# The last step of a graph layer: attention sums in other banks, products by graph, products of ones by ones, and a new written order

## The chip, the cores and the metric

The kernel runs on one core of one Trainium2 chip. The metric is the device time of one execution in microseconds (us); the figure quoted is the median of several runs. Engines are named as the profile names them: PE is TensorE's matmul, PEld its weight load, DVE is VectorE, ACT is ScalarE, POOL is GpSimd and SP is SyncE. L1054 means line 1054 of the kernel.

## The reference

There are 128 graphs of 128 nodes with 1024 features each, all in float32. A layer has two parts, and both add to the features.

```python
def gnn(h, adj, W, a):                       # h: layer norm of x; 16 heads of 64
    Wh = heads(h @ W)
    e = leaky_relu(Wh @ a[:F] + Wh @ a[F:])  # one number for each row and head
    att = softmax(where(adj == 0, -9e15, e)) * adj
    return elu(att @ Wh)

def ffn(x, router_w, down, up):              # x: layer norm again
    gates = softmax over the two largest of (x[:, 0, :] @ router_w.T)   # 8 experts
    d = einsum('blh,erh->bler', x, down)     # rank 16 for each expert
    return x + einsum('bler,ehr,be->blh', d, up, gates)

x = x + gnn(layernorm(x), adj, adj, W, a)
x = x + ffn(layernorm(x), router_w, down, up)
```

Each graph chooses its two experts by its first row alone. The attention weight of a row does not depend on the column except through the mask, so a product with the adjacency matrix followed by a factor for each row and head gives the attention's output.

## The kernel before, in words

**Stages.** Graphs are worked in 64 pairs and in 32 groups of four. The big product with `W` is done for a pair at a time, by a scheme of seven block products named M1 to M7 (a Strassen-like scheme; `a` and `b` behind the name are its column halves). They add up in two double banks of PSUM, `pw0` and `pw1`, which `slot_of(0)` and `slot_of(1)` hand out in turn. For two pairs together, the products with two of the blocks are split once more into inner products, with the code names J0 to J7 and I0 to I7 (L640). DVE and ACT read the banks (`u2`, `u4`, `c21`, `c22`) and POOL adds sums (`ps0` to `ps3` are the sums of a pair's transposed blocks that the next products take as one operand; `eo` and `f` are two more sums).

After the big product come, for each graph, the attention sums (product of `parts` with the adjacency, L770 or, at the end, L1054), the weighing by row (`sums`), the part above zero (`above`), an exponential on ACT and the part below zero (`below`). The graph is then transposed, and the features of a group of four go to the experts: gather the chosen rows of the lower factors (`fe0` to `fe8`, on POOL, L971), lower products (`D`, L986), their gating (`dn`), upper products (`U0` and `U1` for the two halves of the features, L1006) and the final adds (`v...`, L1015), whose results are written out.

**The order.** The kernel runs under a manual schedule: each engine executes its instructions in the order in which the program issues them. That order is written by hand in four lists of codes, FIRST, EVEN, ODD and LAST, one code for a small step. `between` runs a list for a step `q`; a code with `-` belongs to the step before, a code with `+` to the step behind. LAST is the order of the last step, which ends the big product of the last pair and then does all that remains. Moving a code moves all the instructions that it issues, on whatever engine, past the other codes' instructions on the same engines.

**The end.** `at_the_end` (L1039) defines the codes with `+` in LAST. The last two graphs (`i` and `i+1`) are done by halves of the features, so that one half can follow the other from engine to engine. With `r` the graph and `h` the half, the codes are these.

| Code | Function | Engine | What it does |
|---|---|---|---|
| A`rh` | `attend_half` | PE, L1054 | attention sums, two products of 512 columns |
| w`rh`, a`rh`, b`rh` | `weigh_half`, `above_half`, `below_half` | DVE | `sums`, `above`, `below` |
| E`rh` | `exp_half` | ACT | exponential of the sums |
| n`r`, q`r`, s`r` | `mean_of_halves`, `squares_at_end`, `stats_at_end` | POOL, ACT, POOL | mean, squares and deviation of the second layer norm |
| T`rh` | `turn_half` | PE, L1106 | four transposes of 128 columns |
| k`rh`, P`rh` | `keep_half`, `parts_of_half` | ACT, DVE | copy of the transposed half to `y_t`; its first row times the router |

The last group's four graphs go to the experts in two sets. Set A holds the group's first two graphs, which are finished earlier; set C holds the last two. All experts' lower factors are loaded once (`down_all`), so no gather is needed. With `s` the set, `t` the graph in it and `h` the half:

| Code | Function | Engine | What it does |
|---|---|---|---|
| P`s`, R`s` | `parts_of`, `sum_parts` | DVE | product of the first rows with the router, and its sum along the free axis |
| rd`s` | `devs_of` | POOL | the deviations as an operand |
| L`s`, V`s` | `logits_of`, `dev_of` | PE | sums over partitions by a product with ones: logits and deviations |
| ch`s`, sp`s` | `choose_of`, `spread_of` | DVE | the two largest logits, and their difference |
| rt`s`, wg`s` | `ratio_of`, `gates_of` | ACT, DVE | softmax of the two, and the gates |
| d`s` (before: dA, d0C, d1C) | `down_of` | PE, L1210 | lower products, all experts |
| g`s` | `gate_of` | DVE | gating (`dn`) |
| u`ths` | `up_of` | PE, L1224 | upper product, 512 columns |
| m`ths`, v`ths` | `scale_up` and `add_of_scaled` (set A), `add_of_up` (set C) | ACT and POOL, or DVE | scale by the deviation, add to the features, write out |

The steps `m..B` and `v..B` (L1237) do the same scaling and adding for the group before. `aw`, `pe` and `dw` make the attention weights of the two graphs, `join` and `rj` (`rejoin`, L849) put a graph's transposed halves into `y_t`.

**Banks at the end.** Beside `pw0` and `pw1` there is the pool `ps_d` with two double banks. `double` takes one, and waits until the readers of the one that it replaces are done; `single` takes one half of a double. In the kernel before, `attend_half`, `logits_of` and `down_of` all take from `ps_d`; the transposes of half `h` of both graphs go to `slot_of(h)`.

Of the kernel before, what the change touches and what calls it, by code (L numbers as in the profile page):

```python
# [8 lines left out]
F32 = mybir.dt.float32  # L9
# [5 lines left out]
ALU = mybir.AluOpType  # L15
# [32 lines left out]
Jt2- n0- hi0- lo0- J7- J1- q0- ps3- Jt3- Jp- y1- ro1- Jr- I1- n1- t0- J2- Jd- sr- q1- ps2-  # L48
J5- It0- J4- st1- Ja- Js- st0- M7b- J3- It1- M7a- Ip- rj0- Je- rp- c22- I6- ss- L- It2- ch0-
hi3- I7- t1- ch1- It3- fr- M4a- fe4- M4b- jn1- Ir- fe0- c21- lo3- hi2- fe5- Ia- I4- ra- rs-  # L50
fe2- I5- fe1- I2- fe7- Is- I3- lo2- A1 Ie- fe6- Id- hi1- fe3- aw M1b lo1- M1a jn0- pe LW+
# [12 lines left out]
def adj_ffn_kernel(  # L64
# [974 lines left out]
    def at_the_end():  # L1039
# [10 lines left out]
        def attend_half(r, h):  # L1050
            if i + r not in PH:
                PH[i + r] = double("ph")
# [47 lines left out]
        def turn_half(r, h):  # L1100
            if h not in turned:
                turned[h] = slot_of(h)
            pt = turned[h][:, r].rearrange("p (c n) -> p c n", c=CPH)
            for c in range(CPH):
                k = h * CPH + c
                nc.tensor.transpose(pt[:, c], X[i + r][:, k * P:(k + 1) * P], ident)  # L1106

        def keep_half(r, h):
            nc.scalar.copy(y_of(i + r)[:, h * CPH:(h + 1) * CPH],
                           turned[h][:, r].rearrange("p (c n) -> p c n", c=CPH))  # L1110
# [20 lines left out]
        def parts_of_half(r, h):  # L1131
            k = slice(h * CPH, (h + 1) * CPH)
            part = prod_of("C")[:, r:r + 1, :, k]
            rows = turned[h][:, r].rearrange("p (o c n) -> p o n c", o=1, c=CPH)[:, :, 0:1]
# [336 lines left out]
```

## Time and profile before

| What | Value |
|---|---|
| Four runs | 1858.46, 1858.52, 1859.89 and 1861.21 us |
| Median | 1859.21 us |
| Profiled execution, its own time | 1858.78 us |
| Its span | 1856.7 us |
| Mean granted clock of PE | 0.997 |
| Busy: PEld | 1504.7 us (81%) |
| Bytes read and written in HBM | 194.24 and 68.17 MB |

The span goes from the first instruction to the last; the execution's own time contains a little more. In the page's second part, the span is cut into 40 equal slices, and each digit is a busy share, or the granted clock of PE (`PEclk`), in tenths, where 9 stands for nine tenths or more. One slice is 46 us long, so the last digit averages over all that comes after the last big product and some of what lies ahead of it. Parts and groups of instructions are given by line, with the output and the operands by the program's names. In a timeline, a row that covers several records of one kind gives their start, their total length and their number, and in brackets the idle time of the engine ahead of them and what ended it. Tables of stretches give, for each stretch of the span, its length, then the busy time of one engine with the number of its instructions, the granted clock, the DMA engines' share and the GB/s that they moved.

### The profile page before, as it was taken

The page shows a single profiled execution, that of the slowest core. Times are in us where ns is not written, and L with a number is a line of the kernel's source. Part 1 is how long each engine was busy: PE and PEld are TensorE (multiplying, and loading weights), DVE is VectorE, ACT ScalarE, POOL GpSimd, SP SyncE. Part 2 cuts the span into 40 slices and gives each one's busy share as a digit, 9 for nine tenths or more (in the row PEclk, how much of TensorE's full clock was granted, in tenths as well). Part 3 has the DMA queues.
Part 4 walks back from the last instruction along what each step waited for, and adds up shares of the span by engine and source line. Part 5 has one row for each costly group of instructions (what it writes and reads, how often), then busy time and mean ns, then how long its engine had stood idle before and what let it go on. Part 6 is the DMA issues. An engine that isn't in the chain of part 4 may idle for free.

```text
span 1856.7 us, 29668 instructions
## 1 busy us (share of the span) xinstructions
PE 1839.3 (99%) x10196; PEld 1504.7 (81%) x10196; DVE 1580.0 (85%) x3411; ACT 1242.5 (67%) x1423; POOL 1170.4 (63%) x1691
## 2 busy tenths in 40 slices
PE   9999999999999999999999999999999999999997
PEld 6888888888888888888888888888888888888884
DVE  6888888888888888888888888888888888888885
ACT  3666666766666766666666667666667666666676
POOL 3666656667566667566666566675666675666663
PEclk9999999999999999999999999999999999999998
DMA  8455566565575655666655655655665556565443
GB/s 319 153 176 139 186 199 177 184 181 148 183 198 189 182 152 166 194 184 195 175 138 187 199 177 184 179 150 182 194 194 182 148 171 192 184 194 176 134 158 114
DMA packets 349100, 330.42 MB, mean 178 GB/s; under 512 B 279196, under 2 KB 281372, under 8 KB 348440
## 3 DMA queue, kind: packets, MB, share of 16 engines
q1 hardware_dynamic: 331512, 287.09, 51.1%
q0 software_dynamic: 17008, 40.91, 7.4%
q8 instruction: 81, 1.33, 0.3%
q14 instruction: 67, 0.55, 0.1%
q10 hardware_dynamic: 432, 0.53, 0.1%
HBM read 194.24 MB, written 68.17 MB: 141 GB/s over the span
## 4 chain that ended last, share of the span: by engine, by line
PE 92%; POOL 3%; DMA 1%; DVE 1%; issue 1%; ACT 1%; SPq 0%; DVEq 0%; POOLq 0%; ACTq 0%
PE pw L561 58%; PE pw L640 17%; PE ph L770 6%; PE pu L1006 4%; PE pd L986 3%; PE ix L640 3%; POOL down L971 2%; DMA xn<-in_x 1%; DMA w_sb<-in_w 1%; PE pd_all L1210 0%; POOL xt L493 0%; PE pu L1224 0%; ACT ph L802 0%; POOL s L493 0%; PE pl L899 0%
## 5 line engine op out<-in xcount | busy, mean ns | idle before, releaser
L561 PE MATMUL pw<-w_sb,xt 128*128 128x260 f32 (+1 forms) x4080 | 958.6, 385 | 1.0 <-DMA w_sb<-in_w 0.5
L561 PEld LDWEIGHTS pw<-w_sb,xt 128*128 128x128 f32 x4080 | 762.6, 190 | 169.5 <-issue 30.9
L971 POOL DMA_INDIRECT down<-table,at_down x248 | 249.0, 1004 | 197.2 <-DVE of_slot L935 116.0
L708 ACT ACTIVATE parts<-wh,rstd 128x512 fp32r<-128x512 f32 x192 | 135.2, 720 | 344.2 <-DVE wh L568 305.0
L849 ACT COPY y_t<-tt 128x2048 uint16<-128x2048 uint16 x126 | 314.7, 2498 | 1.4 <-DMA tt<-halves 1.4
L561 PE MATMUL pw<-w_sb,s 128*128 128x260 f32 (+1 forms) x1088 | 249.8, 382 | 0.0
L843 ACT COPY halves<-xn 128x2048 uint16<-128x2048 uint16 x126 | 237.5, 1885 | 2.5 <-DVE xn L793 2.0
L561 PEld LDWEIGHTS pw<-w_sb,s 128*128 128x128 f32 x1088 | 206.4, 190 | 34.1 <-DVE wh L568 0.9
L493 POOL TENSOR_TENSOR s<-xt 128x512 f32<-128x512 f32 x64 | 83.2, 1299 | 231.8 <-DMA xt<-in_x_t 231.8
L786 ACT ACTIVATE ph<-ph 128x1024 f32<-128x1024 f32 x126 | 127.9, 1015 | 82.3 <-DVE xn L783 78.7
L1015 DVE SCALAR_TENSOR_TENSOR xn<-pu,rstd,xn 128x512 f32<-128x512 f32 x244 | 168.7, 743 | 11.1 <-PE pu L1006 11.1
L776 DVE TENSOR_TENSOR ph<-ph,att 128x1024 f32<-128x1024 f32 x126 | 149.1, 1228 | 11.1 <-PE ph L770 4.9
L432 DVE BATCH_NORM_STATS2 stats<-xn 128x6 f32<-128x512 f32 x248 | 158.4, 680 | 0.0
L855 ACT ACTIVATE xn<-xn,off,mul 128x1024 f32<-128x1024 f32 x128 | 157.7, 1232 | 0.1
L793 DVE SCALAR_TENSOR_TENSOR xn<-ph,xn 128x1024 f32<-128x1024 f32 x126 | 153.2, 1216 | 0.2
L783 DVE SCALAR_TENSOR_TENSOR xn<-ph,xn 128x1024 f32<-128x1024 f32 x126 | 148.1, 1215 | 0.1
L802 ACT ACTIVATE ph<-xn,acc 128x1024 f32<-128x1024 f32 x126 | 140.9, 1118 | 8.2 <-POOL acc L798 6.3
L712 DVE SCALAR_TENSOR_TENSOR parts<-wh,rstd,parts 128x512 fp32r<-128x512 f32 x192 | 140.3, 744 | 4.2 <-ACT parts L708 0.5
L770 PE MATMUL ph<-parts,adj_f 128*128 128x512 f32 x504 | 142.1, 423 | 0.0
L640 PE MATMUL pw<-w_in,s 128*128 128x260 f32 x496 | 129.2, 383 | 0.0
L640 PE MATMUL pw<-w_sb,i 128*128 128x260 f32 x496 | 129.2, 383 | 0.0
L770 PEld LDWEIGHTS ph<-parts,adj_f 128*128 128x128 f32 x504 | 92.6, 188 | 24.3 <-issue 6.3
(235 smaller groups left out, 2678.3 us busy)
## 6 DMA issues: line engine op xcount, KB each, us to landing
xn<-in_x SPq DMA_DIRECT2D x128, 512.0 KB
xt<-in_x_t SPq DMA_DIRECT2D x127, 512.0 KB
out_y<-xn SPq DMA_DIRECT2D x124, 512.0 KB
adj_f<-in_adj_t POOLq DMA_DIRECT2D x32, 256.0 KB, 7.3
adj_i<-in_adj SPq DMA_DIRECT2D x32, 256.0 KB
down<-table,at_down POOLq DMA_INDIRECT x248, 2.6
w_sb<-in_w SPq DMA_DIRECT2D x3, 1040.0 KB
wt_sb<-in_w_t SPq DMA_DIRECT2D x1, 2048.0 KB
```

Source lines behind the costliest of these rows:

```text
L432: nc.vector.bn_stats(st[:, h, :], X[i][:, h * HALF:(h + 1) * HALF])
L561: nc.tensor.matmul(banks[name][:, j, cols], lhs()[:, k, :], w_sb[:, rhs, k, j, cols], start=(fresh and k == 0), stop=(k == KH - 1), skip_g ...
L640: nc.tensor.matmul(bank(name), sums(lhs)[:, k], w_of[rhs][:, k], start=(fresh and k == 0), stop=(k == KI - 1), skip_group_check=not fresh)
L770: nc.tensor.matmul(PH[i][:, h], GRP[g]["adj_f"][:, t, :], PARTS[q][:, s, NH * (i % 2) + h], start=(s == 0), stop=(s == 1))
L776: nc.vector.tensor_tensor(ph, ph, ATT[i // 2, None][:, i % 2, :, None].to_broadcast([P, H, F]), ALU.mult)
L783: nc.vector.scalar_tensor_tensor(X[i], whole(i), 0.0, X[i], op0=ALU.max, op1=ALU.add)
L793: nc.vector.scalar_tensor_tensor(X[i], whole(i), 1.0, X[i], op0=ALU.min, op1=ALU.add, accum_out=acc[:, 0:1])
L843: nc.scalar.copy(halves, X[i].bitcast(U16).rearrange("p (d s) -> p s d", s=2))
L849: nc.scalar.copy(y_of(i).bitcast(U16).rearrange("p k (n s) -> p s k n", s=2), TT.pop(i).rearrange("p (s k) n -> p s k n", s=2))
L855: nc.scalar.activation(X[i], X[i], AF.Identity, bias=GRP[g]["off"][:, t:t + 1], scale=GRP[g]["mul"][:, t:t + 1])
L971: nc.gpsimd.indirect_dma_start(out=st["down"][:, j * R:(j + 1) * R].rearrange("p r k -> p (r k)"), out_offset=None, in_=table, in_offset=b ...
L1015: nc.vector.scalar_tensor_tensor(y[:, cols], st["pu", h][t], st["rstd"][:, t:t + 1], y[:, cols], op0=ALU.mult, op1=ALU.add)
```

## The change

Five things are changed, all in the last step.

- The attention sums of the last two graphs go to `slot_of(0)` and `slot_of(1)`, where the big products' banks are, and not to the pool `ps_d`. The transposes go to one slot for each graph, not one for each half.
- Logits, deviations and lower products of a set share one double bank: for set A from `ps_d`, for set C `slot_of(0)`. The deviations lie in the second half of it, behind the logits.
- The lower products of set A are issued by graph (`d0A`, `d1A`, 128 columns each) and not for both together (`dA`, 256 columns).
- Two new codes issue products of a matrix of ones by itself (128 columns), whose results nobody reads: `y0+` six of them into the bank that the first transposes take, and `yA+` eight into the bank that the first upper product takes.
- The final adds of set A's second graph are done by DVE in one instruction each, as those of set C are, and not by ACT and POOL. The comparison that makes `hit` moves from the gates to the choice.

The list LAST is written anew with these codes. The order of the inner products, of POOL's gathers and pair sum `ps2`, of M4 and M7 against the lower products D, and of nearly all steps behind them is another one. The lists FIRST, EVEN and ODD stay.

```diff
 LAST = """
-Jt2- n0- hi0- lo0- J7- J1- q0- ps3- Jt3- Jp- y1- ro1- Jr- I1- n1- t0- J2- Jd- sr- q1- ps2-
-J5- It0- J4- st1- Ja- Js- st0- M7b- J3- It1- M7a- Ip- rj0- Je- rp- c22- I6- ss- L- It2- ch0-
...
-aw2 fe8- p1 A0 h1 M2a x1 M2b h0 rj1- x0 e1 eo y1 hi0 sc0 e0 lo0 y0 M6b M6a wg n1 q1 D t0 u2
-u4 f n0 hi1 dn aw0+ lo1 M7a M7b LR+ q0 pe0+ c22 U0 M4b ss t1 hi3 M4a dw0+ v00 rj0 v01 rdA+
-U1 m1B+ lo3 v1B+ m0B+ c21 aw1+ rj1 A00+ pe1+ hi2 A01+ w00+ w01+ v0B+ A11+ a01+ dw1+ a00+
-E01+ jn1 b01+ m2B+ PA+ w11+ lo2 RA+ E00+ T01+ A10+ m3B+ b00+ w10+ n0+ LA+ OA+ a11+ a10+ q0+
-s0+ E11+ VA+ T00+ dA+ E10+ chA+ k00+ b10+ spA+ b11+ k01+ T10+ T11+ n1+ v3B+ rtA+ wgA+ P11+
-k11+ P10+ gA+ u00A+ q1+ P0+ m00A+ RC+ v2B+ LC+ u01A+ jn0 s1+ rdC+ chC+ VC+ m01A+ v00A+ v01A+
-k10+ d1C+ spC+ rtC+ ac u10A+ d0C+ m10A+ wgC+ gC+ u11A+ j1+ u00C+ m11A+ u10C+ j0+ v10A+ u01C+
-v10C+ v00C+ u11C+ v11C+ v01C+ v11A+
+Jt2- Jt3- ps3- hi0- J7- lo0- J1- y1- Jp- J2- ro1- Jr- J4- J5- Jd- sr- t1- st0- n1- M7a- n0-
+Js- It0- J3- Ja- q1- It1- I1- Je- M7b- st1- t0- rp- I6- It2- q0- I7- Ip- ss- It3- L- I2-
...
+fe6- fe0- h0 x0 h1 e0 eo rs- M6a sc0 LR+ hi0 fe4- M6b wg fe3- y0 n0 ps2- lo0 t0 x1 M7b u2 u4
+M7a fe5- e1 q0 f y1 hi1 A00+ c22 aw0+ M4a lo1 t1 n1 hi3 pe0+ q1 lo3 dw0+ M4b c21 A01+ w01+
+OA+ aw1+ w00+ ss D hi2 dn a01+ rj0 a00+ E01+ U0 lo2 v01 A10+ b01+ E00+ pe1+ dw1+ b00+ A11+
+y0+ rdA+ v00 T01+ rj1 U1 w11+ PA+ n0+ T00+ m0B+ m1B+ q0+ RA+ w10+ LA+ k00+ k01+ d1A+ a11+
+v0B+ a10+ E11+ VA+ v1B+ b11+ E10+ m3B+ d0A+ b10+ chA+ T10+ spA+ n1+ T11+ jn1 P10+ m2B+ yA+
+P0+ ac rtA+ q1+ P11+ RC+ wgA+ s1+ gA+ s0+ LC+ u11A+ u01A+ k11+ rdC+ u10A+ k10+ chC+ d0C+ j1+
+v10A+ VC+ spC+ v2B+ jn0 rtC+ u00A+ m00A+ v00A+ v11A+ m01A+ d1C+ v3B+ wgC+ gC+ u10C+ u11C+
+u01C+ v10C+ j0+ u00C+ v00C+ v11C+ v01A+ v01C+
 """.split()
...
         def attend_half(r, h):
             if i + r not in PH:
-                PH[i + r] = double("ph")
+                PH[i + r] = slot_of(r)
...
         def turn_half(r, h):
-            if h not in turned:
-                turned[h] = slot_of(h)
-            pt = turned[h][:, r].rearrange("p (c n) -> p c n", c=CPH)
+            if r not in turned:
+                turned[r] = slot_of(r)
+            pt = turned[r][:, h].rearrange("p (c n) -> p c n", c=CPH)
...
+        def banks_of(s):
+            if ("banks", s) not in got:
+                got["banks", s] = double("banks") if s == "A" else slot_of(0)
+            return got["banks", s]
...
         def logits_of(s):
             n = sets[s][1]
-            got["pl", s] = double("pl")
-            nc.tensor.matmul(got["pl", s][:, 0, 0:n * E], ones, add_of(s)[:, 0:n * E], start=True,
+            nc.tensor.matmul(banks_of(s)[:, 1, 0:n * E], ones, add_of(s)[:, 0:n * E], start=True,
                              stop=True)
...
         def down_of(s, t, n):
-            if ("pd", s) not in got:
-                got["pd", s] = double("pd_all")[:, 0]
             first = sets[s][0] + t
             for k in range(KC):
-                nc.tensor.matmul(got["pd", s][:, t * P:(t + n) * P],
+                nc.tensor.matmul(banks_of(s)[:, 0, t * P:(t + n) * P],
...
+        def stay(n, idle):
+            for _ in range(n):
+                nc.tensor.matmul(idle, ones, ones, start=True, stop=True)
+
+        def stay_before_turn(n):
+            turned[0] = slot_of(0)
+            stay(n, turned[0][:, 0, 0:P])
+
+        def stay_before_up(n):
+            got["pu", "A", 0, 0] = single("pu")
+            stay(n, got["pu", "A", 0, 0][:, 0:P])
...
-        for t in range(2):
-            for h in range(2):
-                does.update({f"m{t}{h}A": (scale_up, "A", t, h)})
+        for h in range(2):
+            does.update({f"m0{h}A": (scale_up, "A", 0, h)})
...
-                    does.update({f"u{t}{h}{s}": (up_of, s, t, h), f"v{t}{h}{s}": (add_of_scaled if s == "A" else add_of_up, s, t, h)})
+                    does.update({f"u{t}{h}{s}": (up_of, s, t, h), f"v{t}{h}{s}": (add_of_scaled if s == "A" and t == 0 else add_of_up, s, t, h)})
```

More of the change, by code (lines that the diff above doesn't have):

```diff
@@ L1133, in parts_of_half @@
             part = prod_of("C")[:, r:r + 1, :, k]
[L1134 removed]
+            rows = turned[r][:, h].rearrange("p (o c n) -> p o n c", o=1, c=CPH)[:, :, 0:1]
             nc.vector.tensor_tensor(part, rows.to_broadcast(part.shape),
@@ L1155, in dev_of @@
             n = sets[s][1]
-            nc.tensor.matmul(got["pl", s][:, 1, 0:n], ones, add_of(s)[:, n * E:], start=True,
+            nc.tensor.matmul(banks_of(s)[:, 1, n * E:n * E + n], ones, add_of(s)[:, n * E:], start=True,
                              stop=True)
@@ L1181, in choose_of @@
             nc.vector.tensor_tensor(pr[:, 0], top[:, 1], top[:, 0], ALU.subtract)
+            hit = got["hit", s] = small.tile([P, n * TOP], F32, tag="own" + s, name="hit", bufs=1)
+            nc.vector.tensor_scalar(hit, val[:, 0].rearrange("p g s -> p (g s)"), own_order, None,
+                                    op0=ALU.is_equal)
         def spread_of(s):
             pr = got["pr", s]
-            nc.vector.tensor_tensor(pr[:, 0], pr[:, 0], got["pl", s][:, 1, 0:sets[s][1]], ALU.mult)
+            n = sets[s][1]
+            nc.vector.tensor_tensor(pr[:, 0], pr[:, 0], banks_of(s)[:, 1, n * E:n * E + n], ALU.mult)
         def ratio_of(s):
@@ L1197, in gates_of @@
             nc.vector.tensor_mul(gate[:, :, 1], pr[:, 1], gate[:, :, 0])
-            val = val.rearrange("p v g s -> p v (g s)")
-            hit = small.tile([P, n * TOP], F32, tag="own", name="hit", bufs=2)
-            nc.vector.tensor_scalar(hit, val[:, 0], own_order, None, op0=ALU.is_equal)
-            nc.vector.tensor_tensor(hit, hit, val[:, 1], ALU.mult)
+            hit = got["hit", s]
+            nc.vector.tensor_tensor(hit, hit, gate.rearrange("p g s -> p (g s)"), ALU.mult)
             gates = got["gate", s] = small.tile([P, n], F32, tag="gate" + s, name="gate_all", bufs=1)
```

18 lines of the change are left out of this document (10 added, 8 removed).

## The prediction

> **What bounds the kernel now.** I read the page first, for the engine that fills the span and for the chain of work that ended last.
>
> ```profile
> PE 1839.3 (99%) x10196; PEld 1504.7 (81%) x10196; DVE 1580.0 (85%) x3411; ACT 1242.5 (67%) x1423; POOL 1170.4 (63%) x1691
> ...
> PEclk9999999999999999999999999999999999999998
> ...
> PE 92%; POOL 3%; DMA 1%; DVE 1%; issue 1%; ACT 1%; SPq 0%; DVEq 0%; POOLq 0%; ACTq 0%
> ```
>
> The matrix engine is the bound for the whole span but its end. The change touches the last step alone, so the second view is the timeline of PE from 1820 us on (start, length, instruction, idle time before it and its releaser).
>
> ```profile
> 1819.74 0.61 PE L1006 MATMUL pu<-up,dn 32*128 32x512 f32 x4
> 1821.70 1.20 PE L1054 MATMUL ph<-parts,adj_f 128*128 128x512 f32 x4 [1.35 <-ACT part_up L1237]
> 1824.37 1.19 PE L1054 MATMUL ph<-parts,adj_f 128*128 128x512 f32 x2 [1.47 <-DVE sums_of L1060]
> 1827.03 1.11 PE L1106 MATMUL pw<-ident,xn 128*128 128x128 f32 x4 [1.47 <-DVE xn L1079]
> ...
> 1830.76 5.31 PE L1210 MATMUL pd_all<-y_t,w_sb 128*128 128x256 f32 x16
> 1835.90 1.04 PE L1106 MATMUL pw<-ident,xn 128*128 128x128 f32 x8
> 1837.70 1.10 PE L1224 MATMUL pu<-w_sb,dn_all 128*128 128x512 f32 x2 [0.76 <-PE pw L1106]
> ...
> 1846.60 4.46 PE L1224 MATMUL pu<-w_sb,dn_all 128*128 128x512 f32 x10
> ```
>
> Up to 1820.35 PE has no gap; after it come three waits of 1.4 us, and a block of 16 lower products that takes 5.3 us. The third view says why those are slow: PE in stretches of 3.41 us (busy, granted clock).
>
> ```profile
> 1820.51:1823.92 3.41, 1.20 (x4) 1.00 0.19 77
> 1823.92:1827.33 3.41, 1.50 (x4) 0.50 0.57 231
> 1827.33:1830.75 3.42, 3.42 (x14) 0.50 0.00 0
> 1830.75:1834.16 3.41, 3.41 (x10) 0.50 0.00 0
> 1834.16:1837.57 3.41, 2.78 (x17) 1.00 0.09 37
> ```
>
> After a stretch with 1.20 us of products (35%) the clock is 0.50 for 10.24 us. A stretch with 2.78 us, 1.9 of them not transposes, keeps it. So at most some 36 us of 1856.7 are open: from 1820.35 to the end. 0.2% is 3.7 us, about what a measurement of this kernel can tell from no change.
>
> **Part 1, up to the last big product.** The order of PE, DVE, ACT, POOL and SP in the built program says who stands behind whom. The inner products (0.88 us a pair of matmuls, by the chain) are reordered: the second joint product now comes right behind the first, and waits for ACT's copy of it (0.38 us) without the filler that stood between, 0.45 us. All that follows fits without a gap, and M6 (s2) ends at 1808.6 as before, since the first attention product of the old order (0.93) is merely elsewhere. M7 may start if pair sum `ps2` is there: on POOL that now stands behind seven gathers, where it was early. A gather takes 1.26 us from start to start; the chosen rows are known at 1794.5, and `eo` (1.30) and the rstd pair (1.0) are in between: `ps2` ends at 1808.4, 0.25 us ahead of need. If the gathers take the 1.42 us of the first one, M7 is 0.9 us late; I take none.
>
> M7 takes 3.70, A00 (half of the 0.93) 0.47, and M4 waits 0.27 for c22's read (0.70), where U0 used to fill. M4 ends at 1816.8, against 1819.27: D (2.16) and U0 (1.07) went behind it. That attention sums now live in pw0 and pw1, not in ps_d, allows this: A00 waits only for M6's readers (done at 1810).
>
> **Part 2, DVE from M4 to the second graph's last half.** From here DVE is laid end to end, at start-to-start distances of the timeline: c21 0.70, sums 0.65, five weights 0.90, sums 0.65, two above 1.28, `lo` 0.72, two L1015 1.36, below 0.75, four divisions 0.88, below 0.75, two L1015 1.36, sums 0.65, product 0.37, reduce 0.30, sums 0.65, two above 1.28: 13.25, to 1830.1. ACT comes out equal: from D's end (1819.4) dn 0.35, y_t 2.5, two exps 1.2, exp 0.2, y_t 2.5, two scalings 1.28, squares 1.25, two copies 1.05, exp 0.56, to 1830.35. Two below (1.5) end at 1831.9.
>
> PE in that time waits for DVE: U0 ends at 1820.9, A10 and A11 start at 1821.75 (behind `lo`), and U1's second half stands behind DVE's fourth L1015, to 1826.8. Lower products of graph A: 32 records of 128 columns in two lots of 16, each 1.8 (the chain's 1.78 for such a lot at full clock), with the logits (0.25) and deviations (0.3): from 1828.2 to 1832.3. Split by graph they cost what 16 records of 256 columns cost at full clock, so the split is free; the clock is not.
>
> **Part 3, choice to end.** The choice of A waits for the end of the last lower product, not of its logits, but DVE is busy to 1831.9 anyway: 0.45 us. Twelve small instructions at 0.2 (`hit` is now the twelfth, and leaves the part behind the exps, so it costs nothing in sum) 2.3, spread 0.17, product parts of C 0.95 (in their shade ACT's two, 0.45), four gates 0.8, dn 0.42: the first upper product starts at 1837.0, against 1837.70. Before, the choice ran beside the lower products; that is where most of the gain from the clock goes.
>
> Then PE: three upper at 0.86 (4.31 us for ten records) to 1839.6, lower 1.8, deviations 0.35, upper 0.86, lower 1.8 to 1844.4. DVE's second add of graph 1 (0.70), which was ACT's and POOL's, waits for ACT's scaling and has C's gates (0.8) and dn (0.42) queued behind it: the last four upper products start at 1845.2, 0.8 late, and end at 1848.7. Three adds of 0.68 follow: 1850.8. The last write: DVE's end to the span's end was 1852.51 to 1856.7, 4.2; as many writes are in flight, so 1855.0.
>
> **The ones products.** Six before the first transposes and eight before the first upper product. A record of 128 columns is 0.11 us at full clock: 12 records 1.3, 16 records 1.8. The first lot runs from 1822.7 to 1824.0, and `below` is ready at 1823.8; U1's second half waits to 1826.8, so it costs nothing. The second needs a bank that ACT frees at 1833.5 and ends at 1835.3, before DVE's reduce at 1835.8: nothing. At half clock they take 2.7 and 3.5 (the opening idle products took 3.97 us for 18, 0.22 each), and the second then delays the logits of C.
>
> **Sum.** 1855.0 is 1.7 below the span of 1856.7. The profiled execution took 1858.78 (2.08 around the span), 0.43 less than the median of 1859.21: 1857.1 for it, 1857.5 as a median.
>
> **Where the clock may still fall.** Behind the first lot of ones come a transpose (0.45), U1's first half (0.55), 1.8 of wait, U1's second half (0.55), a transpose (0.45). A stretch of 3.41 us from 1824.0 holds 1.1 us of products and 0.47 of transposes: between the 35% that fell and the 56 to 81% that did not. Where the stretches begin differs from run to run.
>
> The Trainium skill, "TensorE: Matmul & The Clock Gate", Part 4 (PE-mode transpose), says that a transpose does not count as busy work for the clock gate. By that rule the stretch has 32%, below the row that fell, and the ones stand ahead of the gap that matters: the clock would fall and the time be 1860.6; by the row alone (46%) it stays open. No run here has shown it. The same page, Part 1, gives the window as 3413 ns, which is the grid that the trace shows.
>
> **Rivals.**
> 1. The clock falls once, near 1827.5, and comes back two stretches later at 1834.3, as before: the lower products lose 3.1 us, all on the path. 1860.6. For it: the 35% row and the gap. Against: three of the waits before it are gone.
> 2. Slower: the same fall, but no stretch full enough until 1841, since the stretches in between hold transposes, small products and the wait for a bank. Then the lower products end at 1836.6, the eight ones products run at half clock from 1838.6 to 1842.1, and the logits of C, behind them on PE, come 6 us late; the choice of C decides the end. 1863 to 1866 if the clock is half until the upper products. It decides from the point where the ones end behind DVE's reduce. For it: in the profile a stretch that PE filled (3.42 of 3.42) did not yet bring the clock back. Against: the next one did.
> 3. Faster: the hand-overs are shorter than I laid them, and the last write sees less of its neighbours. In the profile five writes of 256 KB went out within 2.3 us (DMA share 1.04 at 1852); here within 3. Less 0.8 for the write and 1.5 over some sixty hand-overs: 1854.5 to 1855.4.
>
> **How the numbers follow.** The chain as laid, full clock: 0.46 (1855.5 to 1859.5, of which 0.08 below 1855.5). Rival 1: 0.19. Rival 2: 0.16. Rival 3: 0.19. Faster by over 0.2%, below 1855.5: 0.19 + 0.08. Slower, above 1862.9: 0.16 and 0.01 of rival 1. The range runs from rival 3's middle to rival 2's lower end. The likeliest case's own range is 1855.5 to 1859.5: minus 2 for the hand-overs, plus 0.9 for the gathers and 1.1 for waits that I did not see.
>
> **What would show it.** Right: M4 ends near 1816.8; DVE without a gap over 0.5 us from there to 1832; the first upper product near 1837.0; granted clock 1.00 between 1820 and 1850; DVE's end near 1850.8. Wrong: M7 waits for POOL; a clock of 0.50 in the lower products; ones products that end after DVE's reduce for C; a choice that starts more than 0.5 us behind DVE's `below`.

## The result: slower by 0.16%, and the profile after

The changed kernel takes 1862.32 us (median of 40 runs, 1860.06 to 1864.21), the kernel before 1858.89 us (median of 60). The ratio is 1.0016, with a 95% interval from 1.0011 to 1.0020; it is taken over all runs and is not the quotient of the medians, which is 1.0018. Predicted were 1857.5 us. The profiled execution took 1861.85 us with a span of 1860.0 us, 3.3 more than before. First, from the page of the changed kernel, the busy times and the chain of work that ended last, now with 3% of DVE instead of 1%.

```profile
PE 1840.9 (99%) x10240; PEld 1506.6 (81%) x10240; DVE 1581.9 (85%) x3413; ACT 1241.6 (67%) x1421; POOL 1167.0 (63%) x1689
...
PE 91%; POOL 4%; DVE 3%; issue 2%; DMA 1%; ACT 0%; SPq 0%; DVEq 0%; POOLq 0%; ACTq 0%
```

The timeline of PE in the changed kernel, at the places that the prediction named (start, length, instruction, idle time before it and its releaser):

```profile
1817.64 1.98 PE L986 MATMUL pd<-y_t,down 128*32 128x128 f32 x64
...
1822.70 1.50 PE L1228 MATMUL pw<-ones 128*128 128x128 f32 x12
...
1828.87 2.03 PE L1214 MATMUL banks<-y_t,w_sb 128*128 128x128 f32 x16
...
1833.62 1.95 PE L1228 MATMUL pu<-ones 128*128 128x128 f32 x16
1836.14 0.37 PE L1155 MATMUL pw<-add,ones 128*128 128x16 f32 x2 [0.57 <-DVE val L1204]
1837.16 2.84 PE L1241 MATMUL pu<-w_sb,dn_all 128*128 128x512 f32 x6 [0.65 <-DVE dn_all L1223]
...
1842.71 1.95 PE L1214 MATMUL pw<-y_t,w_sb 128*128 128x128 f32 x16
1847.12 5.37 PE L1241 MATMUL pu<-w_sb,dn_all 128*128 128x512 f32 x8 [2.46 <-DVE dn_all L1223]
```

Up to the first upper product nearly all is as it was laid: the lower products of A run at full clock (2.03 us for 16 records), the ones stand in waits, the first upper product starts at 1837.16. The loss is in the last row: a wait of 2.46 us for DVE's `dn`, and then four upper products that take 5.37 us instead of 3.5. PE's stretches show why they are slow (length, busy time, granted clock):

```profile
1843.87:1847.28 3.41, 0.95 (x9) 1.00 0.51 192
1847.28:1850.69 3.41, 3.41 (x5) 0.50 0.31 126
```

The wait leaves 0.95 us of products in one stretch, and the clock is 0.50 in the next. What DVE did meanwhile stands in the chain of waits (start, length):

```profile
1841.91 0.98 PE pu L1241 x2
...
1842.97 0.70 ACT part_up L1254
1843.67 0.02 issue
1843.69 0.75 DVE xn L1247
1844.44 0.09 DVE val L1204
1844.53 0.02 issue
1844.55 0.49 DVE val L1205
1845.04 0.02 issue
1845.06 1.20 DVE hit L1207
1846.26 0.02 issue
1846.28 0.17 DVE gate_all L1209
...
1846.54 0.44 DVE dn_all L1223
1846.98 0.14 issue
1847.12 5.38 PE pu L1241 x8
```

DVE's second add of graph 1 (`v11A`, L1247) waits for ACT's scaling of graph 0 (`m00A`), and C's gates stand behind it in DVE's queue. Two of those gates, on 2 and 4 numbers a partition, take 0.49 and 1.20 us; the same two took 0.16 each for set A. Behind DVE's end (1854.69) the span goes on for 5.3 us.

**A common start.** The opening of the kernel takes up to 2.7 us longer in one execution than in another (last section). So ends are compared below from one place up to which all kernels run the same instructions: the start of the last two graphs' attention products of the step before (L770, at 1766.91 us before and 1767.07 after). "Tail" is from there to the span's end; the other columns count from there too. The last column gives the start and the length of the last upper products: four of C, and a fifth of A in the rows with a star.

| Kernel | Median us | Ratio to before, 95% | Tail | First upper | Last upper |
|---|---|---|---|---|---|
| before | 1858.89 | | 89.79 | 70.79 | 79.69 + 4.46* |
| changed | 1862.32 | 1.0011 to 1.0020 | 92.93 | 70.09 | 80.05 + 5.37 |
| e1: add early | 1859.13 | 0.9988 to 1.0006 | 88.52 | 70.09 | 78.20 + 3.67 |
| e12: other pair of banks | 1860.09 | 0.9995 to 1.0013 | 90.06 | 71.71 | 79.72 + 3.70 |
| e2: POOL's add early | 1860.55 | 0.9995 to 1.0013 | 90.09 | 70.11 | 79.02 + 3.67 |
| e3: ones before the last | 1861.58 | 1.0001 to 1.0019 | 90.31 | 70.09 | 79.95 + 3.70 |
| e9: adds back on POOL | 1863.87 | 1.0014 to 1.0032 | 92.71 | 70.12 | 80.20 + 5.37 |
| e4: before, with ones | 1859.00 | 0.9990 to 1.0008 | 89.40 | 68.84 | 79.39 + 4.46* |
| e5: changed, no ones | 1863.69 | 1.0015 to 1.0032 | 93.02 | 71.30 | 82.68 + 3.67 |
| e6: e1, no first lot | 1860.56 | 0.9995 to 1.0013 | 89.62 | 71.17 | 79.27 + 3.67 |
| e7: e1, no second lot | 1861.11 | 1.0002 to 1.0019 | 89.96 | 70.11 | 79.65 + 3.67 |
| e14: e1, ones inside U1 | 1857.46 | 0.9984 to 1.0002 | 88.52 | 70.08 | 78.19 + 3.67 |
| e8: e1, logits' own bank | 1857.30 | 0.9978 to 0.9996 | 88.19 | 69.79 | 77.89 + 3.67 |
| e10: e8, product between | 1856.68 | 0.9977 to 0.9996 | 87.88 | 69.85 | 76.80 + 4.46* |
| e11: e10, ones inside U1 | 1856.47 | 0.9975 to 0.9994 | 86.92 | 68.88 | 75.83 + 4.46* |
| e13: as e11, other place | 1856.54 | 0.9975 to 0.9993 | 86.90 | 68.88 | 75.82 + 4.46* |

The changed kernel was run 40 times, each experiment 11 times. Each ratio is to the kernel before as it was run beside the experiment (medians from 1858.85 to 1859.25 us). Medians of kernels whose intervals overlap are not set in an order by them alone; the tail is of one profiled execution.

### The profile page after: what moved, and what is told of

Its sections match the earlier page's. It is cut to its first block, busy times and chain, and to the rows that moved or that the text cites. A ratio compares the mean times of both kernels' runs of the same rounds, so it can differ in the third digit from the quotient of the medians.

```text
span 1860.0 us, 29751 instructions
## 1 busy us (share of the span) xinstructions
PE 1840.9 (99%) x10240; PEld 1506.6 (81%) x10240; DVE 1581.9 (85%) x3413; ACT 1241.6 (67%) x1421; POOL 1167.0 (63%) x1689
## 3 DMA queue, kind: packets, MB, share of 16 engines
q8 instruction: 82, 1.34, 0.3%
## 4 chain that ended last, share of the span: by engine, by line
PE 91%; POOL 4%; DVE 3%; issue 2%; DMA 1%; ACT 0%; SPq 0%; DVEq 0%; POOLq 0%; ACTq 0%
PE pw L561 57%; PE pw L640 17%; PE ph L770 6%; PE pu L1006 3%; PE pd L986 3%; PE ix L640 3%; POOL down L971 2%; DMA w_sb<-in_w 1%; POOL s L493 1%; PE pu L1241 0%; POOL xt L493 0%; ACT ph L802 0%; DVE w_sb L1310 0%; DVE w_sb L306 0%; PE pl L899 0%
## 5 line engine op out<-in xcount | busy, mean ns | idle before, releaser
L770 PE MATMUL ph<-parts,adj_f 128*128 128x512 f32 x504 | 142.0, 423 | 0.0
L770 PEld LDWEIGHTS ph<-parts,adj_f 128*128 128x128 f32 x504 | 92.6, 188 | 24.2 <-issue 6.3
```

The source lines that it names most:

```text
L770: nc.tensor.matmul(PH[i][:, h], GRP[g]["adj_f"][:, t, :], PARTS[q][:, s, NH * (i % 2) + h], start=(s == 0), stop=(s == 1))
```

## Experiments

**e1, the add early.** DVE does `v11A` right behind `v10A`, ahead of C's spread; nothing else moves but the write that it starts.

```diff
-v10A+ VC+ spC+ v2B+ jn0 rtC+ u00A+ m00A+ v00A+ v11A+ m01A+ d1C+ v3B+ wgC+ gC+ u10C+ u11C+
+v10A+ VC+ jn0 v11A+ spC+ v2B+ rtC+ u00A+ m00A+ v00A+ m01A+ d1C+ v3B+ wgC+ gC+ u10C+ u11C+
```

> Edit of the changed kernel: DVE's second add of graph 1 (v11A) is put ahead of C's spread, so that C's gates no longer stand behind it. Theory 1 (the loss of the changed kernel is this queue: the add waits for ACT's scaling until 1843.69, the gates follow, POOL's adds then hold two of them, and the gap of 2.46 us ahead of the last upper products empties a stretch of the clock): the gates are done by 1843.5, the last upper products start near 1845.2 instead of 1847.1 and run at full clock (3.5 us for 8 records, not 5.4); span 3 to 4 us below 1860.0, time 1858.0 to 1859.5. Theory 2 (the clock falls at the end anyway, since the products behind 1843 leave gaps whatever DVE does): start 1.9 us earlier, but still over 5 us for the last eight records, time near 1860.5. Theory 3 (the last writes set the end, 5.3 us from DVE's end to the span's end): under 1 us gained.

Measured: 1859.13 us, 3.2 below the changed kernel; tail 88.52, 4.4 below. DVE's timeline in this kernel (all its times are 1.7 us later than in the profile above, by the opening):

```profile
1841.75 1.41 DVE L1247 SCALAR_TENSOR_TENSOR xn<-pu,rstd,xn 128x512 f32<-128x512 f32 x2 [0.73 <-PE pu L1241]
...
1844.52 0.16 DVE L1205 TENSOR_TENSOR val<-pr,val 128x2 f32<-128x2 f32 x1
1844.71 0.16 DVE L1207 TENSOR_TENSOR hit<-hit,val 128x4 f32<-128x4 f32 x1
...
1846.41 0.42 DVE L1223 TENSOR_TENSOR dn_all<-pw,gate_all 128x256 f32<-128x256 f32 x1 [1.34 <-PE pw L1214]
```

Both adds run in time that DVE had free, the gates are done at 1845.07, and `dn` now waits 1.34 us for PE and not PE for it. The last four products start 1.85 us earlier and run at full clock. Theory 1 holds, counted from the common start; the other two fall.

**e12, another pair of banks.** Why did the add wait for ACT? It reads one half of a double bank; the other half holds the product that ACT scales (the ones of `yA` take the half of `u00A`, which PE computes fourth and not first, and the first one computed, `u11A`, gets the half beside it). Two upper products change places, so that ACT's two share a double bank and DVE's two share the other.

```diff
-P0+ ac rtA+ q1+ P11+ RC+ wgA+ s1+ gA+ s0+ LC+ u11A+ u01A+ k11+ rdC+ u10A+ k10+ chC+ d0C+ j1+
+P0+ ac rtA+ q1+ P11+ RC+ wgA+ s1+ gA+ s0+ LC+ u01A+ u11A+ k11+ rdC+ u10A+ k10+ chC+ d0C+ j1+
```

> Edit of the changed kernel: two of A's upper products change places (u01A ahead of u11A), so that the one which DVE adds late shares its double bank with the other one that DVE adds, and not with the one that ACT scales; the order of DVE's instructions is untouched. Theory 1 (the add waits for ACT only because the two halves of one double bank are kept in order by the program): the add runs near 1842.1, the gates behind it are done by 1843.9, and the last upper products start near 1845.2 as in e1: time 1859.1. Theory 2 (its place in the queue itself is what costs, whatever it waits for): a start near 1847, time 1862.3.

```profile
1844.93 0.16 DVE L1193 TENSOR_TENSOR pr<-pr,pw 128x2 f32<-128x2 f32 x1 [1.15 <-PE pw L1160]
1845.00 0.74 DVE L1247 SCALAR_TENSOR_TENSOR xn<-pu,rstd,xn 128x512 f32<-128x512 f32 x1
1845.66 0.16 DVE L1204 RECIPROCAL val<-val 128x2 f32<-128x2 f32 x1
1845.86 0.16 DVE L1205 TENSOR_TENSOR val<-pr,val 128x2 f32<-128x2 f32 x1
```

In DVE's timeline the add follows the spread without a wait, in an unchanged queue, and the gates take 0.16 each. From the first upper product to the last four it is 8.01 us, as in e1 (8.11), against 9.96 in the changed kernel. So the wait came from the shared double bank, whose two halves the built program keeps in order: in the trace the add waits on a semaphore of ACT in the changed kernel, and on none of ACT's here. The median is 1860.09 where 1859.1 was expected: in this profile the clock fell already in A's lower products (first upper at 71.71), a point that e14 takes up.

**e2, POOL's add early.** DVE's queue stays; POOL does `v3B` in its idle time, so that one of its three adds leaves the time of C's gates.

```diff
-v10A+ VC+ spC+ v2B+ jn0 rtC+ u00A+ m00A+ v00A+ v11A+ m01A+ d1C+ v3B+ wgC+ gC+ u10C+ u11C+
+v10A+ VC+ spC+ v2B+ v3B+ jn0 rtC+ u00A+ m00A+ v00A+ v11A+ m01A+ d1C+ wgC+ gC+ u10C+ u11C+
```

> Edit of the changed kernel: POOL's add v3B stands right behind v2B, in POOL's idle time, and not behind v00A; DVE's order is untouched. Theory 1 (a DVE product of two operands in SBUF waits until POOL's running add is done; in the changed kernel the two small ones took 0.47 and 1.19 us against 0.16 elsewhere, each ending with an add of POOL): the second of them takes 0.2 us, C's gates end about 1 us earlier, the last upper products start near 1846.0, time about 1861. Theory 2 (the two small ones are slow for another reason): their durations and the start at 1847.1 stay, time 1862.3.

DVE's and then POOL's timeline of this kernel:

```profile
1846.70 0.47 DVE L1205 TENSOR_TENSOR val<-pr,val 128x2 f32<-128x2 f32 x1
1847.21 0.16 DVE L1207 TENSOR_TENSOR hit<-hit,val 128x4 f32<-128x4 f32 x1
```

```profile
1845.89 1.27 POOL L1264 TENSOR_TENSOR xn<-part_up,xn 128x512 f32<-128x512 f32 x1 [0.68 <-ACT part_up L1254]
...
1847.79 1.26 POOL L1264 TENSOR_TENSOR xn<-part_up,xn 128x512 f32<-128x512 f32 x1 [0.63 <-ACT part_up L1254]
```

The first product of two small operands starts while POOL adds (1845.89 to 1847.16) and ends with it, at 1847.17; the second runs while POOL is idle and takes 0.16. In the changed kernel POOL's three adds ran without a gap from 1843.74 (3.71 us in all, 1.24 each), and the two ended at 1845.02 and 1846.25, with the first and the second add. DVE's adds, which take one operand from a bank, ran beside POOL at 0.75. The Trainium skill, "SBUF — State Buffer", section "SBUF: two separate sides", states this: a DVE instruction with two operands in SBUF and a GpSimd instruction that reads SBUF share a pair of ports, and the later one waits for the whole of the other. The measured ends agree, to 0.02 us. The last products start 1.0 us earlier, as expected, and the shorter wait (1.43 us) left them at full clock.

**e3, ones before the last products.** Ten products of ones in the wait of 2.46 us.

```diff
+        def stay_before_last(n):
+            got["pu", "C", 1, 0] = single("pu")
+            stay(n, got["pu", "C", 1, 0][:, 0:P])
...
-v10A+ VC+ spC+ v2B+ jn0 rtC+ u00A+ m00A+ v00A+ v11A+ m01A+ d1C+ v3B+ wgC+ gC+ u10C+ u11C+
+v10A+ VC+ spC+ v2B+ jn0 rtC+ u00A+ m00A+ v00A+ v11A+ m01A+ d1C+ yC+ v3B+ wgC+ gC+ u10C+ u11C+
```

> Edit of the changed kernel: ten more products of ones by ones (2.2 us at full clock) between C's last lower product and the last upper products, in the bank that the upper products take. Their results are not read. Theory 1 (the clock falls because the stretch ahead is empty; PE waits there for DVE anyway): the start at 1847.1 stays, the granted clock is 1.00 to the end, the eight records take 3.5 us instead of 5.4, time about 1860.4. Theory 2 (products of ones do not hold the clock, or delay what stands behind them): eight records over 5 us, or a start behind 1847.5, time 1862.3 or more.

The start is the same (79.95), the last four take 3.70 us, the granted clock is 1.00 up to the span's last part. The tail is 2.6 below the changed kernel's: 1.7 by the clock, 0.9 by a shorter last write. The median is only 0.74 lower (1860.4 us was expected), and the intervals of the two ratios overlap. So the clock's part of the loss is 1.7 us in a profile where the fall meets all four products; how much it is over all executions is not shown.

**e9, the adds back on ACT and POOL.** This undoes one part of the change, and puts POOL's `v2B` and `v3B` ahead.

```diff
-v10A+ VC+ spC+ v2B+ jn0 rtC+ u00A+ m00A+ v00A+ v11A+ m01A+ d1C+ v3B+ wgC+ gC+ u10C+ u11C+
+v2B+ m10A+ v10A+ VC+ spC+ v3B+ jn0 rtC+ u00A+ m00A+ v00A+ m11A+ v11A+ m01A+ d1C+ wgC+ gC+ u10C+ u11C+
...
-                    does.update({f"u{t}{h}{s}": (up_of, s, t, h), f"v{t}{h}{s}": (add_of_scaled if s == "A" and t == 0 else add_of_up, s, t, h)})
+                    does.update({f"u{t}{h}{s}": (up_of, s, t, h), f"v{t}{h}{s}": (add_of_scaled if s == "A" else add_of_up, s, t, h)})
```

> Edit of the changed kernel: the second graph's adds of set A go back to ACT (scaling) and POOL (adding), as in the kernel before, with v2B and v3B ahead of them on POOL; DVE's queue holds none of them. Theory 1 (DVE's queue behind that add is the loss): C's gates are done near 1843.5, the last upper products start 1.5 to 1.9 us earlier than in the changed kernel, at full clock; time 1858.5 to 1860.5. Theory 2 (five adds of 1.25 us on POOL with two buffers for the scaled halves take its place: the banks come free late): the last upper products start as late as now, time 1861.5 to 1863.

1863.87 us, above what either theory expected, and the last products start as late as in the changed kernel, but by another road. Now ACT's queue is the one that waits: the scaling of `m10A` waits 1.98 us for POOL to free a buffer, the ratio of C comes behind it, 1.5 us later than in the changed kernel (76.5 against 75.1 from the common start), and five adds of POOL then hold DVE's two small products for 0.91 and 1.19 us. That DVE does these adds is not what costs; where the add stands and what it shares does.

**e4, the kernel before with ones.** Six products of ones in each of its three waits of 1.4 us.

```diff
-U1 m1B+ lo3 v1B+ m0B+ c21 aw1+ rj1 A00+ pe1+ hi2 A01+ w00+ w01+ v0B+ A11+ a01+ dw1+ a00+
-E01+ jn1 b01+ m2B+ PA+ w11+ lo2 RA+ E00+ T01+ A10+ m3B+ b00+ w10+ n0+ LA+ OA+ a11+ a10+ q0+
+U1 m1B+ lo3 v1B+ m0B+ c21 aw1+ rj1 y0+ A00+ pe1+ hi2 A01+ w00+ w01+ v0B+ y0+ A11+ a01+ dw1+ a00+
+E01+ jn1 b01+ m2B+ PA+ w11+ lo2 RA+ E00+ y0+ T01+ A10+ m3B+ b00+ w10+ n0+ LA+ OA+ a11+ a10+ q0+
```

> Edit of the kernel before: three times six products of ones by ones in PE's three waits of 1.4 us (ahead of the first and the third pair of attention products and ahead of the first transposes), nothing else. Their results are not read. Theory 1 (the clock of 0.50 from 1823.9 to 1834.2 is on the path, and the ones hold it up): no stretch below 0.9 between 1820 and 1846, the block of lower products takes 3.6 us instead of 5.3, time 2 to 3.5 us below the kernel before: 1855.5 to 1857. Theory 2 (the products at half clock are hidden behind DVE): the clock is up and the time stays within 1 us. Theory 3 (the ones do not count): clock and time as before.

The clock is up from 1819 to 1842, the first upper product comes 1.95 us earlier than before. But the tail is only 0.4 shorter: the clock then falls at the next gap, to 0.50 from 1842.48 to 1845.89, and 16 lower products of C take 3.29 us instead of 2.05. The fall had moved, not gone, so the 2 to 3.5 us of theory 1 did not come. The changed kernel did the same, one place further on.

**e5, e6, e7, the ones left out.** In the changed kernel both lots, in e1 either lot; the banks are taken as before.

```diff
-            does.update({"y0": (stay_before_turn, 6), "yA": (stay_before_up, 8)})
+            does.update({"y0": (stay_before_turn, 0), "yA": (stay_before_up, 0)})
```

> Edit of the changed kernel: both lots of products of ones by ones have zero products; the banks are taken as before. Theory 1 (the ones hold the clock up and stand in PE's waits): without them the stretches ahead of the transposes and of the first upper product hold about 1.5 and 1.0 us of products of 3.41, the clock falls at least once between 1826 and 1841, and the time rises by 1.5 to 4 us over the changed kernel's: 1864 to 1866. Theory 2 (the changed order alone keeps PE busy enough): clock 1.00 up to 1843, time as the changed kernel's, 1862.3. Theory 3 (the ones are in the way): a gain of up to 1 us.

> Edit of the kernel with the second add of graph 1 put early (1859.1 us): the first lot of ones (y0, six products ahead of the transposes) has zero products. Theory 1 (the first lot holds the clock for the lower products of A): a stretch of 0.5 behind 1826, the first upper product 1 to 3 us later than 70.1 us behind the last whole attention products of the step before, time 1860 to 1862. Theory 2 (not needed): 1859.1.

> Edit of the kernel with the second add of graph 1 put early (1859.1 us): the second lot of ones (yA, eight products ahead of the first upper product) has zero products. Theory 1 (the second lot holds the clock for the upper products and C's lower products): half clock in the upper products behind 1840, C's lower products 2 us longer, time 1860.5 to 1862. Theory 2 (not needed): 1859.1.

Without the first lot (e6) the clock falls in A's lower products (2.92 us for 16), and the tail grows by 1.1 us; without the second (e7) it falls in the upper products (4.28 us for six records, 2.84 with the ones), and the tail grows by 1.4. C's lower products, expected 2 us longer in e7, ran at full clock. Medians rise by 1.4 and 2.0. Without both, in the changed kernel (e5), it falls at both places and not at the end, so the profile's tail is the same; the median is 1.4 higher, at 1863.69 just below the 1864 to 1866 expected. The ones cost nothing, as predicted: the first upper product starts at 70.11 without the second lot and at 70.09 with it. They hold the clock, but the first lot not always: of the nine profiles that have it and none inside U1, the clock fell in A's lower products in three (e8, e10, e12).

**e8, a bank for the logits.** DVE stood idle for 1.27 us before the choice of A, since logits and lower products share a double bank. In this kernel A's logits go to `pw1`, free between the last attention sums and the last transposes.

```diff
+            got["pl", s] = slot_of(1) if s == "A" else banks_of(s)
-            nc.tensor.matmul(banks_of(s)[:, 1, 0:n * E], ones, add_of(s)[:, 0:n * E], start=True,
+            nc.tensor.matmul(got["pl", s][:, 1, 0:n * E], ones, add_of(s)[:, 0:n * E], start=True,
...
-            lg = banks_of(s)[:, 1, 0:n * E].rearrange("p (g e) -> p g e", g=n)
+            lg = got["pl", s][:, 1, 0:n * E].rearrange("p (g e) -> p g e", g=n)
...
-y0+ rdA+ v00 T01+ rj1 U1 w11+ PA+ n0+ T00+ m0B+ m1B+ q0+ RA+ w10+ LA+ k00+ k01+ d1A+ a11+
+y0+ rdA+ v00 T01+ rj1 U1 w11+ PA+ n0+ T00+ m0B+ m1B+ q0+ RA+ w10+ k00+ k01+ d1A+ LA+ a11+
```

> Edit of the kernel with the second add of graph 1 put early (1859.1 us): the logits of A get a bank of their own (pw1, between the attention sums and the transposes of the last graph) and are issued behind the first graph's lower products. Theory 1 (sharing one bank with the lower products makes DVE wait 1.27 us for the choice of A, on the path): the wait is gone, the first upper product starts 68.9 us behind the last whole attention products of the step before instead of 70.1, time 1858.0. Theory 2 (the choice is early, but C's row sums, behind the transposes, or the ones products in PE's queue, take the place of the wait): the first upper product is 0.5 us early at most, time 1858.8 to 1859.2.

The wait is gone, but the first upper product is only 0.3 us earlier, since the clock fell in A's lower products in this profile (2.83 us for 16). 1857.30 us, where the theories had 1858.0 and 1858.8 to 1859.2; its interval lies below 1. The profiled execution took 1859.17, so what a usual one gains is not seen in it.

**e10, an upper product between.** One upper product of A (`u01A`) stands behind C's second lower product, where PE waited 0.61 us for `dn`; `u10A` and `u00A` move up into its place.

```diff
-P0+ ac rtA+ q1+ P11+ RC+ wgA+ s1+ gA+ s0+ LC+ u11A+ u01A+ k11+ rdC+ u10A+ k10+ chC+ d0C+ j1+
-v10A+ VC+ jn0 v11A+ spC+ v2B+ rtC+ u00A+ m00A+ v00A+ m01A+ d1C+ v3B+ wgC+ gC+ u10C+ u11C+
+P0+ ac rtA+ q1+ P11+ RC+ wgA+ s1+ gA+ s0+ LC+ u11A+ u10A+ k11+ rdC+ u00A+ k10+ chC+ d0C+ j1+
+v10A+ VC+ jn0 v11A+ spC+ v2B+ rtC+ m00A+ v00A+ d1C+ u01A+ wgC+ gC+ v3B+ m01A+ u10C+ u11C+
```

> Edit of the kernel with A's logits in a bank of their own (1857.3 us): one upper product of A (u01A, 0.95 us) is put on PE behind C's second lower product, where PE waits 0.61 us for DVE's dn. Theory 1 (PE is without a gap from the first upper product to its end, so the wait is worth its length): the last upper products start 0.6 us earlier after as much work, time 1856.7. Theory 2 (the bank of that product is read late, and the third of the last four waits for it, or DVE is the later one): 1857.3 or more.

1856.68 us; PE goes without a gap from that lower product to its end. The gain in the tail is 0.3, since another wait of 0.34 us, for DVE's spread, has come up ahead of that lower product.

**e11, e13, e14, ones inside U1.** The upper products `U1` of the group before wait 0.97 us between their two halves. Four products of ones are put there, in e11 and e13 on e10, in e14 on e1. In e11 they write over a part of a transposed half that is read later, so that its results are wrong and only its times can be used; in e13 and e14 the place is written again before it is read.

```diff
-... T01+ rj1 U1 w11+ PA+ ...
+... T01+ rj1 Ua+ y1+ Ub+ w11+ PA+ ...
```

> Edit of the kernel of e10 (expected at 1856.7 us): four more products of ones by ones between the two halves of U1, where PE waits 0.97 us for DVE. Their results are not read. Theory 1 (the stretch from the transposes to U1's end is what lets the clock fall in some executions): clock 1.00 from 1820 to the last upper products in the profile and less spread; median 0.3 to 0.8 us below e10. Theory 2 (it falls anyway or the ones delay U1): as e10 or more.

> Edit of the kernel with the second add of graph 1 put early (e1, 1859.1 us): four more products of ones by ones between the two halves of U1, where PE waits 0.97 us for DVE. Their results are not read. Theory 1 (the stretch with that wait lets the clock fall in about half of the executions, which costs 1.1 to 1.6 us each time): clock 1.00 up to the last upper products, median 0.4 to 0.8 us below e1, so 1858.4 to 1858.8. Theory 2 (the fall has another cause): the same median as e1, 1859.1, and a fall in the profile in as many cases.

> Edit of the kernel of e10 (1856.7 us): the same four products of ones by ones between the two halves of U1. Theory 1: the first upper product 1.0 us earlier than in e10, as the profile of e11 had it (68.9 us behind the last whole attention products of the step before, not 69.85), median 1856.0 to 1856.4. Theory 2: 1856.7.

With them the clock is 1.00 up to the end of PE in the profiles of e11, e13 and e14. In e13 the first upper product is 0.97 earlier than in e10 (68.88 against 69.85), and the tail is 86.90, the shortest of all. The medians hardly follow: e11 is 0.2 us and e13 0.1 us below e10, where 0.3 to 0.8 and 0.3 to 0.7 were expected. e14 gives 1857.46 where e1 gave 1859.13, more than the 0.4 to 0.8 expected; the intervals overlap, and its profile has the same tail as e1's, in which the clock had not fallen. So how often the clock falls there, and what that costs over all executions, stays open.

Kernels with the same instructions up to A's lower products had a fall there in three profiles (e8, e10, e12) and none in the changed kernel, e1, e2, e3, e7 and e9. What differs is where the stretches begin. The stretch of the changed kernel and that of e10, and the one behind each:

```profile
1823.39:1826.80 3.41, 2.44 (x18) 1.00 0.00 0
1826.80:1830.21 3.41, 3.14 (x22) 1.00 0.40 161
```

```profile
1824.84:1828.25 3.41, 2.44 (x13) 1.00 0.00 0
1828.25:1831.66 3.41, 3.41 (x19) 0.50 0.77 308
```

Both are busy for 2.44 us, and only the second loses the clock. By the timelines, the first holds some 0.8 us of ones (128 rows) and 1.3 of U1 (32 rows a product), the second almost nothing of 128 rows but transposes, and 1.9 of U1. A closer pair is e1 (kept) and e8 (lost):

```profile
1825.45:1828.86 3.41, 2.43 (x14) 1.00 0.00 0
1828.86:1832.28 3.42, 3.14 (x25) 1.00 0.51 202
```

```profile
1826.08:1829.50 3.42, 2.44 (x15) 1.00 0.00 0
1829.50:1832.91 3.41, 3.41 (x16) 0.50 0.57 227
```

Here the transposes are equal too (0.60 us); e1 has 0.44 us of ones and 1.62 of U1, e8 0.25 and 1.82. A shift of 0.2 us decides. That products of 32 rows count for less fits these pairs, but it is argued, not shown: where in the stretch the idle time lies differs as well. The busy share alone does not decide: 1.75 us of upper products (51%) kept the clock in the changed kernel (1850.73 to 1854.14), and 2.08 (61%, of which 0.38 are products of 2 columns) lost it in e4 (1839.07 to 1842.48).

e13 beats both kernels: 1856.54 us, 0.07 to 0.25% below the kernel before by its interval.

## Why the prediction was wrong

The median lay inside the range, but on the other side of the kernel before: 1.7 us less was forecast, and 3.4 more came (by the medians). Its steps, from the common start (predicted, measured): M7's start 41.73 and 41.93, M4's end 49.9 and 50.2, D 50.3 and 50.6, the first upper product 70.09 and 70.09. Behind it the two part: the last four upper products 78.3 and 80.05, PE's end 81.8 and 85.4, DVE's end 83.9 and 87.6, the span's end 88.1 and 92.9. e1, with one instruction moved, has 78.2, 81.9, 84.1 and 88.5: that is the predicted chain.

**Right.** POOL's `ps2` ended at 1808.71, 0.3 us ahead of M7, which had no gap. M4 went ahead of D as said, the attention sums' new banks made no wait. DVE's chain from M4 to the choice had one gap of 1.27 us, which is the choice's wait for the last lower product; it was in the sum as 0.45, and smaller terms that were laid too long made up for it. So the sign "a choice that starts more than 0.5 us behind DVE's `below`" was there, and that 70.09 was met to the hundredth is luck. So is part of the clock up to there: e12, with the same instructions ahead of its first upper product, lost it and came to 71.71. The ones cost nothing (e5 to e7).

**Wrong, the first term.** "DVE's second add of graph 1 (0.70), which was ACT's and POOL's, waits for ACT's scaling and has C's gates (0.8) and dn (0.42) queued behind it: the last four upper products start at 1845.2, 0.8 late". The queue was seen and mis-sized: 1847.12. From the common start this is 1.8 us late. Of these, 1.2 are C's gates, 2.0 us instead of 0.8 (1844.44 to 1846.45), because POOL's three adds run beside them; the rest came in hand-overs and in a scaling that started 0.2 late, which the text had not laid one by one. That the add waits for ACT at all, though DVE needs nothing of ACT's result, comes from the shared double bank (e12); the prediction had the wait and not its reason. I had taken 0.2 us for each small instruction from rows where POOL was idle. The profile of before had the sign: there L1197, the product that is now L1205, took 0.85 us and ended at 1843.44, when POOL's adds ended (1843.42).

```profile
1840.94 2.48 POOL L1247 TENSOR_TENSOR xn<-part_up,xn 128x512 f32<-128x512 f32 x2
...
1842.59 0.85 DVE L1197 TENSOR_TENSOR val<-pr,val 128x2 f32<-128x2 f32 x1
```

**Wrong, the second term.** "granted clock 1.00 between 1820 and 1850". I looked for a fall only behind the first lot of ones. A wait of 2.46 us for DVE leaves 0.95 us of products in a stretch (28%), less than the 35% that had already fallen in the profile of before. It costs 1.9 us (5.37 against the 3.5 laid; 1.7 against the 3.67 and 3.70 of e1 and e3). The two terms are one cause: e1 takes both away.

**Wrong, the third term.** The last write was taken from before at 4.2 us, and was 5.31. In thirteen of the sixteen profiles it is 4.1 to 4.5; it is longer here, in e2 (5.19) and in e9 (4.93). In these three SP's issue of `v01A`'s write lasts 1.64, 1.45 and 1.11 us; it is SP's last, and in the other thirteen profiles SP's last issue lasts 0.38 to 0.41. So the delay is in the issue of a write; what holds it is not settled.

The sum: 1.8 + 1.9 + 1.1 is 4.8 of the 4.8 us between the predicted and the measured tail. e1 brings back 4.4 of them, the longer write included.

**The rivals.** The slower rival had a similar time, but its mechanism, a half clock until the ones of `yA` and late logits of C, was not there: the logits follow DVE's reduce at 1836.14. Rival 1, a single fall in A's lower products, is what e6, e8, e10 and e12 show, at 1 to 1.6 us and not 3.1, since the clock is back within one stretch. Of the two readings weighed there (transposes counted or not), the two pairs of stretches shown under e14 decide for neither; the half of U1 which the prediction took as 0.55 us lasts 1.13. A row of the profile before speaks for the rule of the Trainium skill ("TensorE: Matmul & The Clock Gate", Part 4): its stretch of 3.42 us that was full, partly with transposes, did not bring the clock back. A row of e4 speaks against taking it as nothing at all:

```profile
1835.65:1839.07 3.42, 2.25 (x12) 1.00 0.13 51
1839.07:1842.48 3.41, 2.08 (x9) 1.00 0.64 256
```

The first of these holds 1.03 us of transposes and 1.2 of other products (36%), and the clock stays at 1.00 in the next, while 1.20 us (35%) in the profile before and 1.31 (38%; e1, 1849.34 to 1852.76), without transposes, lost it.

## What to carry to other kernels

Look at what an instruction in a queue waits for before counting what stands behind it, and at which banks it shares: here exchanging two products that share a double bank freed the queue without moving it. Price small DVE instructions on SBUF by what POOL does in that moment. When a gap is closed with products that only hold the clock, look for the next gap: in e4 and in the changed kernel the fall moved there.

## What was not expected of the hardware

- **The opening.** The first 16 products behind the idle ones took 3.69 us in the profiles of before and after, 5.46 in e1, 5.69 in e2, 5.57 in e3 and 5.20 in e4, with the granted clock at 1.00 in the table of stretches throughout. But that table counts time without a clock record as 1.00, and the trace's first record of 1.00 begins at 4.62 us in before, 4.12 in after, and at 9.56, 9.92, 9.74 and 9.52 in e1 to e4, in the midst of these products. An estimate with half speed up to that record, 3.69 plus half the time from the first product (5.98, 5.88, 5.93 and 6.48 us) to the record, gives 5.48, 5.71, 5.59 and 5.21 us: the measured lengths to 0.02. So the opening is longer by the clock. The common start lies between 1766.68 (e14) and 1769.39 us (e3). This is the same size as the whole effect of the change; without a common start, profiles of such kernels can't be compared by their spans.
- **U1 in halves.** The eight records of U1 together took 1.14 us (before); split by a wait, four take 1.13 us, twice (after). Here the split of products of 32 rows cost as much again as the whole.
- **A small product held for 1.20 us.** In the changed kernel DVE's product on 4 numbers a partition ended with POOL's add on 512; in e2, with POOL idle, it took 0.16.
